# Two transformer layers on one core: second head's contexts of 19 steps turned by transfers, output products moved behind the next step's first projection

## The chip, the core and the metric

The kernel runs on one core of a Trainium2 chip. A core has five engines that run side by side, each taking its own instructions in order: TensorE (PE, matrix products and transposes; its weight loads are listed apart as PEld), VectorE (DVE), ScalarE (ACT), GpSimd (POOL) and SyncE (SP). SP does nothing here but start transfers; ACT and POOL can start transfers too. Transfers run on 16 DMA engines that all queues share. The metric is the device time of one execution in microseconds (us), lower is better. The kernel before takes 1981.68 us, the median of three runs (1981.44, 1981.68 and 1984.95).

## The reference, cut to what matters

Two layers, each `x = x + attention(layernorm(x)) + experts(layernorm(x))`, on 4 sequences of 512 tokens with 512 channels, all in float32. The change lies in the first layer, mostly in its attention:

```
q  = rope(rmsnorm(xn @ Wq))                  # 16 heads of 128
lk = rope(rmsnorm(xn @ Wlk)); lv = xn @ Wlv  # keys and values of the token's own window
ck, cv = compressed keys and values, one entry per 4 tokens
sc = q . ck                                  # only the 8 largest of each row are kept
ctx = (softmax(top8(sc)) @ cv + softmax(window(q . lk)) @ lv) / 2
out = concat_heads(ctx) @ Wo
...
ffn: each token goes to the 2 of 8 experts with the largest router logits
```

The output product `ctx @ Wo` sums over head and channel, so a context, which comes out with tokens on the partitions, has to be turned (channels on the partitions) before it can be the stationary operand of that product.

## The kernel before, in words

**Steps.** The first layer's attention runs in 32 steps `i`, one for each pair of heads `g` (8 of them) and sequence `b` (4). A step does the scores, the top 8, the contexts and the output products of its two heads, and beside them the projections of step `i + 1` (queries, keys and values, seven products in place of eight, after Strassen and Winograd). The main loop writes this by hand in program order:

- `scores(i, 0)`: compressed scores `sp` (L845), window scores `st` (L856), then exponentials (L860) on ACT, a mask (L864) on POOL and the top-8 chain (L848 to L880) on DVE. Then `turn_keys(1)` (L772).
- `first()` of the next step's projection: four products (L734, left operand from `wA`), their adds (L782, L788), then `finish(0)`: squares on ACT (L601), powers on POOL (L606), rotation on DVE (L613 to L616), scaling on ACT (L752).
- `scores(i, 1)`; `turn` of the first head's scores (L890, copies L891 and L892 on ACT); `second`; `context(i, 0)` (L906 to L924); `third`; `context(i, 1)`; `fourth` and `fifth`; the output products; and between them, at places `(i, h)`, jobs of other parts.

**Turning by PE or by transfer.** `turn_context` turns a context with four PE transposes (L931) into PSUM and copies it to `cT` on ACT (L932). From step 5 on the first head's context and half of the queries are turned by transfers instead: `split_halves` (L692, ACT, 1046 ns) parts each float32 into its high and low 16 bits, `store_halves` (L698) writes 256 KB to DRAM, and `load_halves` (L702) brings it back with a transposing transfer. The split tiles and the contexts share a tag `ctx` with two buffers.

**Output.** In steps 5 to 23 `output7` computes the output products of a step, again with seven products for eight (L970, 28 instructions), with four sums on DVE (L991 to L997) and seven adds into `acc` (L981). Its first part `before` is product x of the first head alone; `rest` starts with product y, which needs the second head. In the other steps `output` does it plainly (L939, L942). `load_out` (L108) loads `Wo` of a pair of heads into the only buffer, `combine_out` prepares the sums of `Wo` for `output7`.

**Other work in the steps.** Places in steps 2 to 4 hold the routing and, for every token tile `n` (16), `load_whole` (L1082), `part_halves` (L1087, ACT copy `xh<-xw`) and `store_parts` (L1090), which write the normalized rows to DRAM in halves. Places of steps 5 to 22 hold the experts, two blocks of 128 rows per step: `fetch_halves` (L524, POOL gathers the rows `xr`), `store_halves` of the experts (L529, `xrd`), `load_turned` (L534, transposing load `xT`), `fetch` (L489, POOL gathers the expert's weights `we`), `apply` (products L552, add L555, store `yd` L561). The last eight blocks hold two half blocks of 64 rows with an expert each and so fetch two sets of weights. In steps 29 to 31 the second layer's normalization of tiles 0 to 11 runs in the steps too (`next_layer`: L230 to L250, POOL add L1149, store of `acc` L1150).

**What sets the order.** The framework lays out each engine's instructions by a simulated timetable: it takes what it believes ready, the earlier in program order first. `tc.keep_in_program_order(x)` pins `x` behind the instruction written before it on the same engine; later instructions may still pass it. Transfers wait for their data at the head of the issuing queue, and everything behind them in that queue waits too. In these steps the projections and output products draw on three PSUM banks (`mm`), scores and contexts on three (`sc`).

Of the kernel before, what the change touches and what calls it, by code (L numbers as in the profile page):

```python
# [50 lines left out]
def two_layers(ctx: ExitStack, tc: tile.TileContext, a: dict, out: bass.AP, large: bass.AP):  # L51
# [54 lines left out]
    def load_out(g):  # L106
        wo = wpool.tile([P, HG, HID], F32, tag="Wo", name=f"Wo_{g}", bufs=1)
        nc.sync.dma_start(out=wo, in_=a["Wo"][ds(g * HG * D, HG * D), :].rearrange("(h p) c -> p h c", p=P))  # L108
        return wo
# [111 lines left out]
        tc.keep_in_program_order(V.memset(turned, 1.0))  # L221
        V.tensor_scalar(turned[R:P, :], wcol[R:P, 0:1], wcol[R:P, 1:2], D * math.sqrt(D), ALU.mult, ALU.mult)

    def layernorm(n, pool, bank, scaled=False, bufs=None):

# [13 lines left out]
        def rows():  # L241
            tag = "ctx" if n in (2, 3) else "xn"
            xn = made["xn"] = (wk0 if n in (2, 3) else pool).tile([P, HID], F32, tag=tag, name=f"xn_{n}", bufs=bufs)
            if scaled:
                pin(A.activation(xn, acc[:, n, :], AF.Identity, scale=mv[:, 1:2], bias=mv[:, 0:1]))
            else:
                made_ = V.tensor_scalar(xn, acc[:, n, :], mv[:, 0:1], mv[:, 1:2], ALU.subtract, ALU.mult)
                if n < TC or n + 1 == NT:
                    tc.keep_in_program_order(made_)
            (nc.scalar if TC <= n < 2 * TC else nc.sync).dma_start(out=xnd[ts(n, P), :], in_=xn)  # L250

        def turn():
            xn, tr = made["xn"], bank("tr", f"trx_{n}")
# [336 lines left out]
    for t_ in cv0s:  # L590
        G.memset(t_, 0.0)
        G.memset(t_[96:P, D : D + 1], 2.0)

    def squares(x, heads, pool, name, extra=1.0, use="k"):

# [436 lines left out]
    def first_logits(b):  # L1032
        def get(rows_):
            V.tensor_reduce(lg0[:, ts(b, TC), :], rows_[:, :, 1:, :], AX.X, ALU.add)
        row_w[b], turn = logits(b, wr, 1 + E, sp0, "r0", get, psum)
        return turn
# [41 lines left out]
    whole = {}  # L1078

    def load_whole(n):  # L1080
        x = whole[n] = rout["halves"].tile([P, HID], F32, tag="xw", name=f"xw_{n}", bufs=4)
        nc.sync.dma_start(out=x, in_=xnd[ts(n, P), :])  # L1082

    def part_halves(n):
        x = whole[n]
        xh = whole[n] = rout["halves"].tile([P, 2, HID], U16, tag="xh", name=f"xh_{n}", bufs=4)
        A.copy(xh, x.bitcast(U16).rearrange("p (d h) -> p h d", h=2))  # L1087

    def store_parts(n):
        tc.keep_in_program_order(nc.sync.dma_start(out=xhd[ts(n, P)], in_=whole.pop(n)))  # L1090
# [29 lines left out]
    for b, place in enumerate(((3, 4), (4, 0), (4, 1), (4, 2), (4, 3))):  # L1120
        if b:
            jobs0.append((place, lambda b=b: rout["r"].list(b - 1)))
        if b < B:
            jobs0.append((place, lambda b=b: rout["r"].mark(b)))
    there = [(2, 4)] + [(3, h) for h in (0, 1, 2, 3, 3.5, 4)] + [(4, h) for h in (0, 1, 2)]
    for n in range(NT):
        k = n // 2
        for d, f in enumerate((load_whole, part_halves, store_parts)):
            jobs0.append((there[k + d], lambda n=n, f=f: f(n)))
    jobs0.append(((4, 3), begin_experts))  # L1130
    jobs0.append(((4, 3.5), lambda: rout["ex"].store_halves(0)))
    jobs0.append(((4, 3.5), lambda: rout["ex"].fetch_halves(1)))
# [8 lines left out]
            jobs0.append((at[2 * i + 1], lambda i=i: rout["ex"].fetch(i + 1)))  # L1141
        jobs0.append((at[2 * i + 1], lambda i=i: rout["ex"].store_halves(i + 2)))
    def next_layer(n, pool, bank):
        make_rows, turn_ = layernorm(n, pool, bank, bufs=2 if bank is psum else TC)

        def rows():
            make_rows()

            G.tensor_tensor(acc[:, n, :], acc[:, n, :], rout["wo_b"], ALU.add)  # L1149
            nc.sync.dma_start(out=accd[ts(n, P), :], in_=acc[:, n, :])  # L1150
        return rows, turn_

    v = {}
# [129 lines left out]
    start[7][0]()  # L1283
    start[7][1]()
    first_logits(1)()
    for i, (g, b) in enumerate(steps):
        if b == 0:
            if g:
                out_w[g] = load_out(g)
            if g + 1 < NH // HG:  # L1290
                groups[g + 1] = load_later(g + 1)
        more = i + 1 < len(steps)
        turn_last = turn_keys
        now = qkT
        cT = qp.tile([P, HG, S], F32, tag="cT", name=f"cT_{g}_{b}", bufs=1)
        nc.sync.dma_start(out=cv0s[i % 2][96:P, 0:D], in_=cv[0:32, b, 0:D])
        em0, lT0 = scores(i, 0, now, (lambda: (turn_last(1), next(comp[0]))) if i == 0 else None)
        if i:
            turn_last(1)
        if more:  # L1300
            load_sums(i + 1)
            qkT, sums_x, first, second, third, fourth, fifth, turn_queries, turn_keys, _ = project(i + 1)
            first()
            sums_x()
            if b == 2 and g + 1 in groups:
                groups[g + 1][0][0] = load_block(g + 1, "wA")
        run0((i, 0))
        em1, lT1 = scores(i, 1, now)
        if i == 0:
            second(0)  # L1310
# [29 lines left out]
        if i >= 5:  # L1340
            load_halves(cT[:, 0:1, :].bitcast(U16), halves_c)
        ctx1 = context(i, 1, lT1, sT1, lv)
        if i < 5:
            turn_context(i, 0, ctx0, cT)
        if i == 5 or b == 0 and 5 < i < 24:
# [2 lines left out]
        if more:  # L1348
            fourth()


            if 5 <= i < 24:
                turn_queries(1)
                turn_keys(0)
                fifth()
            else:
                fifth()
        seven = 5 <= i < 24
        if seven:
            before, rest_ = output7(i, cT)  # L1360
            before()
        turn_context(i, 1, ctx1, cT)
        if more and not 5 <= i < 24:
            turn_queries(1)
            turn_keys(0)
        run0((i, 3.5))
        if seven:
            rest_()
        else:
            for t in range(TC):  # L1370
                output(i, t, cT)
        run0((i, 4))
# [1116 lines left out]
```

## Time and profile before

| what | value |
|---|---|
| median of 3 runs | 1981.68 us (1981.44 to 1984.95) |
| profiled execution | 1975.01 us, its span 1973.2 us |
| granted TensorE clock | 0.999 of full speed |
| PE busy | 1933.4 us, 98% of the span |
| DVE busy | 1481.5 us, 75% |
| ACT busy | 892.8 us, 45% |
| POOL busy | 756.1 us, 38% |
| context transposes L931 | 148 instructions, 23.7 us busy, 275 ns mean |
| `cT<-trc` copies L932 | 37, 576 ns mean |
| splits `halves_c<-ctx` L692 | 27, 1046 ns mean |
| transposing loads of `cT` L702 | 27, 3.2 us from issue to landing (median) |
| sum of PE's idle time, 300 to 1090 us (steps 5 to 23) | 7.35 of 790 us |

Steps 5 to 23 fill the time from about 280 to 1090 us, with a step every 43.1 us where nothing is disturbed. A busy time on PE is a latency from an instruction's start to its modelled end; instructions overlap, so how long PE is held by one is read from the start of the next. A bracket behind an instruction gives the time that its engine sat idle before it and what ended that. DMA rows give the time from issue to landing.

### The profile page before, as it was taken

The numbers are of one execution on the slowest core, as the hardware profiler recorded it, in microseconds if no ns is written. First come the engines' busy times: TensorE is split into PE (matmuls) and PEld (weight loads), VectorE is DVE, ScalarE is ACT, GpSimd is POOL, SyncE is SP. The second block draws the span as 40 slices with busy tenths as digits, with TensorE's granted clock in tenths as the row PEclk, the third lists the DMA queues.
The fourth block names the chain that finished last, engine by engine and source line by source line (L and its number), as shares of the span: only waits on it lengthen the run. The fifth ranks groups of instructions, "written<-read, shape, count | busy, mean of one in ns | idle before, by whom it ended". The sixth has DMA issues, their size and how long they took to land.

```text
span 1973.2 us, 28229 instructions
## 1 busy us (share of the span) xinstructions
PE 1933.4 (98%) x9010; PEld 1206.8 (61%) x9010; DVE 1481.5 (75%) x3662; ACT 892.8 (45%) x2650; POOL 756.1 (38%) x827
## 2 busy tenths in 40 slices
PE   7999999999999999999999999999999999999998
PEld 4676667776677677766667776666434445445443
DVE  7778878786776777776668888888796655666886
ACT  5556654444444444444445455455233433333332
POOL 5423244443433333344332454455114432333551
PEclk9999999999999999999999999999999999999999
DMA  9214366654666575567663433333317775775541
GB/s 293 104 61 142 130 176 180 198 155 144 186 191 167 172 204 152 147 184 223 221 223 98 121 109 109 95 113 105 122 53 257 256 256 191 277 251 175 158 154 67
DMA packets 224589, 326.51 MB, mean 165 GB/s; under 512 B 110384, under 2 KB 144304, under 8 KB 212656
## 3 DMA queue, kind: packets, MB, share of 16 engines
q1 hardware_dynamic: 196208, 173.60, 30.3%
q0 software_dynamic: 27072, 148.91, 22.4%
q10 hardware_dynamic: 1152, 2.10, 0.3%
q8 instruction: 74, 1.21, 0.3%
q14 instruction: 83, 0.68, 0.1%
HBM read 230.44 MB, written 70.25 MB: 152 GB/s over the span
## 4 chain that ended last, share of the span: by engine, by line
PE 79%; DVE 10%; DMA 4%; ACT 3%; issue 2%; POOL 1%; SPq 0%; DVEq 0%; ACTq 0%; POOLq 0%
PE p L734 23%; PE hp_r L552 12%; PE op L939 4%; PE st L856 4%; PE st L1522 3%; PE po L1660 3%; PE cx L1536 3%; PE qp L1498 3%; PE sp L845 2%; PE ox L970 2%; PE o L1605 2%; DMA halvesd_q<-halves_q 2%; PE oz L970 1%; PE ca L908 1%; PE trk L772 1%
## 5 line engine op out<-in xcount | busy, mean ns | idle before, releaser
L552 PE MATMUL hp_r<-we_r,xT_r 128*128 128x512 f32 (+1 forms) x592 | 226.4, 596 | 1.2 <-DMA we_r<-in_Wh,wrow_r 0.8
L606 POOL TENSOR_TENSOR ss_q<-ss_q,nhalf 128x4 f32<-128x4 f32 x64 | 70.9, 1108 | 375.0 <-ACT ss_q L603 375.0
L864 POOL TENSOR_TENSOR lT<-lT,lmask 128x512 f32<-128x512 f32 (+1 forms) x128 | 150.7, 1191 | 102.9 <-ACT lT L860 101.8
L734 PE MATMUL p<-wT,x 128*128 128x384 f32 x512 | 176.6, 488 | 2.6 <-DVE u L800 1.5
L734 PE MATMUL p<-wB,x 128*128 128x384 f32 x512 | 176.9, 490 | 1.3 <-DVE u L814 1.0
L734 PE MATMUL p<-wA,xnT 128*128 128x384 f32 x512 | 173.6, 490 | 1.0 <-DVE u L782 1.0
L860 ACT ACTIVATE lT<-st,ss_k 128x256 f32<-128x256 f32 (+1 forms) x256 | 98.8, 441 | 158.6 <-PE st L856 155.4
L1524 ACT ACTIVATE pT<-st 128x1024 f32<-128x1024 f32 x128 | 123.4, 1016 | 59.6 <-PE st L1522 51.1
L552 PEld LDWEIGHTS hp_r<-we_r,xT_r 128*128 128x128 f32 (+1 forms) x592 | 83.6, 170 | 98.2 <-issue 92.8
L734 PEld LDWEIGHTS p<-wB,x 128*128 128x128 f32 x512 | 94.0, 191 | 64.7 <-issue 8.8
L734 PEld LDWEIGHTS p<-wT,x 128*128 128x128 f32 x512 | 93.4, 190 | 64.9 <-DVE s L880 4.8
L734 PEld LDWEIGHTS p<-wA,xnT 128*128 128x128 f32 x512 | 95.1, 192 | 60.8 <-DVE u L782 2.8
L601 ACT ACTIVATE sq_q<-qb 128x128 f32<-128x128 f32 x256 | 79.2, 310 | 96.4 <-DVE qb L788 53.0
L856 PE MATMUL st<-qkT 128*128 128x256 f32 (+1 forms) x512 | 114.6, 353 | 0.0
L569 POOL DMA_INDIRECT row_r<-yd,slot_r x64 | 72.5, 1133 | 74.5 <-DMA yd<-yr_r 21.8
L856 PEld LDWEIGHTS st<-qkT 128*128 128x128 f32 x512 | 92.2, 190 | 11.5 <-issue 1.8
L939 PE MATMUL op<-Wo,cT 128*128 128x512 f32 x208 | 92.8, 593 | 0.0
L752 ACT ACTIVATE qb<-qb,ss_q 128x128 f32<-128x128 f32 x256 | 81.8, 392 | 21.3 <-POOL ss_k L605 16.0
L606 POOL TENSOR_TENSOR ss_k<-ss_k,nhalf 128x2 f32<-128x2 f32 (+1 forms) x96 | 86.7, 903 | 8.0
L734 PE MATMUL p<-wT,xnT 128*128 128x384 f32 x256 | 88.2, 487 | 0.3 <-DVE wT L121 0.3
L489 POOL DMA_INDIRECT xr_r<-xnd,rows_r x36 | 40.5, 1125 | 120.6 <-PE trm_r L540 88.4
L922 ACT ACTIVATE ctx<-cb,sums 128x128 f32<-128x128 f32 x128 | 39.7, 360 | 101.0 <-DVE sums L918 93.6
(390 smaller groups left out, 4558.5 us busy)
## 6 DMA issues: line engine op xcount, KB each, us to landing
x<-xsd SPq DMA_DIRECT2D x112, 256.0 KB, 5.1
yd<-yr_r SPq DMA_DIRECT2D x72, 256.0 KB, 5.4
xrd_r<-xr_r SPq DMA_DIRECT2D x36, 256.0 KB, 2.3
halvesd_c<-halves_c SPq DMA_DIRECT2D x27, 256.0 KB, 3.5
halvesd_q<-halves_q SPq DMA_DIRECT2D x26, 256.0 KB, 2.9
wA<-in_wA SPq DMA_DIRECT2D x16, 384.0 KB, 3.8
wB<-in_wB SPq DMA_DIRECT2D x16, 384.0 KB, 6.8
xnd<-xn SPq DMA_DIRECT2D x24, 256.0 KB, 2.0
```

Source lines behind the costliest of these rows:

```text
L552: PE.matmul(hp[ts(h, m), :], lhsT=xT[:, k, ts(h, m)], rhs=w[:, ts(k, HID)], start=(k == 0), stop=(k == KC - 1))
L569: G.indirect_dma_start(out=x, out_offset=None, in_=self.yd, in_offset=at_rows(self.r.slot[:, k, n : n + 1]))
L601: pin(A.activation(sq, x[:, h, :], AF.Square, accum_out=ss[:, j : j + 1]))
L606: pin(G.tensor_tensor(ss, ss, nhalf[:, 0:n], ALU.pow))
L734: fixed(PE.matmul(p, lhsT=x[:, k, ts(c, P)], rhs=w[:, k, :], start=(k == 0), stop=(k == 1)))
L752: A.activation(x[:, j, :], x[:, j, :], AF.Copy, scale=scale[:, n : n + 1])
L856: PE.matmul(st[:, ds((t % 2) * 256, n)], lhsT=qkT[:, HG + h, ts(t, P)], rhs=qkT[:, h, ds(t * P, n)], start=True, stop=True)
L860: A.activation(lT[:, ds(half * 512 + c * 256, n)], st[:, ds(c * 256, n)], AF.Exp, scale=norm_k[(i, h)][2 * half + c])
L864: G.tensor_tensor(dst, dst, lmask.rearrange("p a w j -> p (a w j)")[:, 0:n], ALU.mult)
L939: PE.matmul(op, lhsT=cT[:, h, ts(t, P)], rhs=wo[:, h, :], start=(h == 0), stop=(h == HG - 1))
L970: PE.matmul(p[:, ts(c, 256)], lhsT=left[:, ts(c, P)], rhs=right, start=new and c == 0, stop=True, skip_group_check=True)
L1524: A.activation(pt[:, ts(pair, 2), :], st, AF.Exp, scale=SCALE1)
```

## The change

From step 5 to 23 the second head's context is split on ACT (`c1`), stored and loaded back turned into `cT[:, 1]`, as the first head's already was. The products of `output7` and the load that they need are kept in a list `before_this` and put behind the next step's `first()`. `load_out` goes behind them. The 16 KB copy of the first compressed entries is written behind `first()` for the next step (from step 4 on), just ahead of the transposing load. `xw` and `xh` of tiles 0 to 5 are worked in steps 1 and 2 in an earlier pool, the others in steps 2 to 4, and the ACT copies are pinned. In steps 29 to 31 the two stores of `next_layer` are issued by ACT.

```
-    def layernorm(n, pool, bank, scaled=False, bufs=None):
+    def layernorm(n, pool, bank, scaled=False, bufs=None, on_scalar=False):
...
-            (nc.scalar if TC <= n < 2 * TC else nc.sync).dma_start(out=xnd[ts(n, P), :], in_=xn)
+            (nc.scalar if TC <= n < 2 * TC or on_scalar else nc.sync).dma_start(out=xnd[ts(n, P), :], in_=xn)
...
+    def load_first_entries(i):
+        nc.sync.dma_start(out=cv0s[i % 2][96:P, 0:D], in_=cv[0:32, steps[i][1], 0:D])
...
     def load_whole(n):
-        x = whole[n] = rout["halves"].tile([P, HID], F32, tag="xw", name=f"xw_{n}", bufs=4)
+        x = whole[n] = (rout["halves"] if n >= 6 else sp0).tile([P, HID], F32, tag="xw", name=f"xw_{n}", bufs=4 if n >= 6 else 2)
...
-        A.copy(xh, x.bitcast(U16).rearrange("p (d h) -> p h d", h=2))
+        tc.keep_in_program_order(A.copy(xh, x.bitcast(U16).rearrange("p (d h) -> p h d", h=2)))
...
-    there = [(2, 4)] + [(3, h) for h in (0, 1, 2, 3, 3.5, 4)] + [(4, h) for h in (0, 1, 2)]
+    there = [((1, 4), (2, 0), (2, 1)), ((2, 0), (2, 1), (2, 2)), ((2, 1), (2, 2), (2, 3)), ((2, 4), (3, 0), (3, 1)),
+             ((3, 0), (3, 1), (3, 2)), ((3, 1), (3, 2), (3, 3)), ((3, 4), (4, 0), (4, 1)), ((4, 0), (4, 1), (4, 2))]
     for n in range(NT):
-        k = n // 2
-        for d, f in enumerate((load_whole, part_halves, store_parts)):
-            jobs0.append((there[k + d], lambda n=n, f=f: f(n)))
+        for place, f in zip(there[n // 2], (load_whole, part_halves, store_parts)):
+            jobs0.append((place, lambda n=n, f=f: f(n)))
...
-        make_rows, turn_ = layernorm(n, pool, bank, bufs=2 if bank is psum else TC)
+        make_rows, turn_ = layernorm(n, pool, bank, bufs=2 if bank is psum else TC, on_scalar=bank is psum)
...
-            nc.sync.dma_start(out=accd[ts(n, P), :], in_=acc[:, n, :])
+            (nc.scalar if bank is psum else nc.sync).dma_start(out=accd[ts(n, P), :], in_=acc[:, n, :])
...
+    before_this = []
     for i, (g, b) in enumerate(steps):
         if b == 0:
-            if g:
-                out_w[g] = load_out(g)
...
-        cT = qp.tile([P, HG, S], F32, tag="cT", name=f"cT_{g}_{b}", bufs=1)
-        nc.sync.dma_start(out=cv0s[i % 2][96:P, 0:D], in_=cv[0:32, b, 0:D])
+        if i < 5:
+            load_first_entries(i)
...
+            if i >= 4:
+                load_first_entries(i + 1)
+        if before_this:
+            load_halves(cT[:, 1:2, :].bitcast(U16), before_this[0])
+        for f in before_this[1:]:
+            f()
+        before_this = []
+        cT = qp.tile([P, HG, S], F32, tag="cT", name=f"cT_{g}_{b}", bufs=1)
         run0((i, 0))
+        if g and b == 0:
+            out_w[g] = load_out(g)
...
         ctx1 = context(i, 1, lT1, sT1, lv)
+        seven = 5 <= i < 24
+        if seven:
+            halves_c = split_halves(f"c1_{i}", ctx1.bitcast(U16).rearrange("p n (f x) -> p n x f", x=2))
...
         if seven:
-            before, rest_ = output7(i, cT)
-            before()
-        turn_context(i, 1, ctx1, cT)
-        if more and not 5 <= i < 24:
-            turn_queries(1)
-            turn_keys(0)
+            before_this = [store_halves(f"c1_{i}", halves_c), *output7(i, cT)]
+        else:
+            turn_context(i, 1, ctx1, cT)
+            if more:
+                turn_queries(1)
+                turn_keys(0)
         run0((i, 3.5))
-        if seven:
-            rest_()
-        else:
+        if not seven:
             for t in range(TC):
                 output(i, t, cT)
```

## The prediction

> **What bounds the kernel now.** I read the page first, then the stretch of steps 5 to 23 by windows, the PE's timeline over one turn from step to step, and last the PE's own waits.
>
> The page's busy list and chain, and the window of steps 5 to 23 (columns: stretch, length, then PE, PEld, DVE, ACT, POOL busy with counts, clock, DMA share, GB/s):
>
> ```profile
> PE 1933.4 (98%) x9010; PEld 1206.8 (61%) x9010; DVE 1481.5 (75%) x3662; ACT 892.8 (45%) x2650; POOL 756.1 (38%) x827
> ...
> PE 79%; DVE 10%; DMA 4%; ACT 3%; issue 2%; POOL 1%; SPq 0%; DVEq 0%; ACTq 0%; POOLq 0%
> ...
> 300.00:1090.00 790.00, 782.65 (x3653) 551.96 (x3652) 595.31 (x1616) 362.75 (x1269) 296.20 (x315) 1.00 0.60 177
> ```
>
> PE idles 7.35 of 790 us at full clock: every instruction taken from PE there shortens the kernel, every new PE wait lengthens it. The turn from step 12 to 13 (start, length, instruction):
>
> ```profile
> 602.57 2.75 PE L734 MATMUL p<-wB,x 128*128 128x384 f32 x8
> 605.15 1.03 PE L970 MATMUL ox<-Wo,cT 128*128 128x256 f32 x4
> 606.01 0.60 PE L931 MATMUL trc<-ident,ctx 128*128 128x128 f32 x4
> 606.45 1.06 PE L845 MATMUL sp<-ckT,qkT 128*128 128x32 f32 x8
> ...
> 614.48 5.33 PE L734 MATMUL p<-wA,xnT 128*128 128x384 f32 x16
> ```
>
> The second head's four transposes hold PE from 606.01 to 606.45, and PE goes on without a gap. The PE waits that matter (in brackets):
>
> ```profile
> 211.95 0.33 PE L931 MATMUL trc<-ident,ctx 128*128 128x128 f32 x1 [2.38 <-DVE ctx L924]
> ...
> 465.33 0.71 PE L911 MATMUL cb<-cv,sT 96*128 96x129 f32 x4 [1.27 <-ACT sT L891]
> ...
> 990.79 0.71 PE L911 MATMUL cb<-cv,sT 96*128 96x129 f32 x4 [2.17 <-ACT sT L891]
> ...
> 1305.27 0.63 PE L255 MATMUL trx<-ident,xn 128*128 128x128 f32 x4 [3.55 <-DVE xn L247]
> ```
>
> **Transposes removed.** 19 x 4. The L931 row says 275 ns each, and the Trainium skill ("TensorE: Matmul & The Clock Gate", Part 4: PE-mode transpose) also gives about 275 ns in a kernel; that would be 76 x 0.275 = 20.9 us. But this is a latency: start to start, four take 0.44 us. So 19 x 0.435 = **-8.3 us**, and the timeline decides, since PE is full. The copy out of PSUM (0.57 us, ACT) goes; a split into halves (1.05 us, the L692 row) comes. It starts when ctx1 is done at 599.5, in an ACT gap of 3.47 us before 602.33: nothing.
>
> **The transfers.** Frame: that same turn. SP's queue:
>
> ```profile
> 600.13 0.34 SPq L561 DMA_DIRECT2D yd<-yr_r  x1
> 601.10 0.34 SPq L529 DMA_DIRECT2D xrd_r<-xr_r  x1
> 601.89 3.77 SPq L685 DMA_DIRECT2D x<-xsd  x2
> 607.70 1.27 SPq L534 DMA_TRANSPOSE xT_r<-xrd_r  x1
> ```
>
> The new store is pinned behind xrd: issue about 601.5, some 1.2 us after POOL's weight gather began at 600.37. Stores whose issue ends up to 0.94 us after a gather's start land in 2 to 4 us; those ending 0.97 to 1.6 after it land with the gather, in 6.2, 6.7 and 7.4 us (xrd at 385.2, 298.7, 730.4). The Trainium skill ("DMA: Bandwidth & Descriptors", Queues, rings and completion order) says that a DMA engine round-robins between rings by packet, which would let a small store through in about 3 us; its remark that a completion waits for that engine's earlier writes in all queues fits the slow rows better. I take the rows: landed near 608.2, then the transposing load at the cT row's median 3.2 us: **611.4**. SP sits at its wait meanwhile; behind it are the x loads (next read over 20 us later) and xT_r (landing about 614, read at 621.6).
>
> Who needs it: product y. After fifth's end at 605.15 come sp 0.89, st 1.52, keys 0.44, first 5.16 and product x 0.86: **614.0**. Slack 2.6 us, no wait in steps with one weight gather per expert. In steps 18 to 21 a second gather (half experts) delays stores to 8.9 and 10.1 us (xrd at 952.8 and 999.1); there the data come up to 2 us late: +2.5 us in all (ends 0 and +6). By the packet rule it would be 0, and the sum 2.5 lower.
>
> **The products moved.** Same 28 instructions, 6.0 us, now behind first. Their DVE work (seven adds, four sums, 6.3 us) moves from 606-614 to 613-622. DVE must then do some 13.0 us in the 15.2 us up to 628.4 (products 6.3, rotation 1.5, second head's top-8 chain 3.1, the rest 2.1), while the first head's chain runs earlier, uncovered. Full, not over: +1 us in all (ends 0 and +10). Wo's load, now behind the products, waits at SP until about 619 instead of 613; nothing follows it before 626.7, its reader combine_out is later still. The first-entry copies (16 KB, 2.2 us) sit ahead of the transposing load and are ready early: nothing.
>
> **What moves with it on POOL.** The row gather (L524) is pinned behind the pow of first's finish, which comes 6.5 us earlier, so the gather goes from 624.4 to about 617.8 and xrd no longer waits for it:
>
> ```profile
> SPq L529 <- DMA xr_r<-xhd,rows_r: 35.5, 30, 2.6
> ...
> ACT halves_c L692 <- DMA halvesd_q<-halves_q: 22.1, 4, 6.2
> ```
>
> The second row is the cause of the four PE waits at L911 (6.0 us): the query store landed with the weight gather, ACT held the split and sT behind it. From the four, PE waits once that store lands more than about 14.7 us after the first head's score transposes (463.9 - 448.05 = 15.8 gave 1.27). After the change it issues 1.4 us earlier, but so does the gather, and the store ends about 1.0 us after the gather's start, on the border. If slow, it lands 7.1 to 9.3 us after 626.4, by 635.7; the limit is 621.6 + 14.7 = 636.3. So no new wait, and most old ones go: **-5.0 us** (ends 0 and -6.0).
>
> **Step 3.** Twelve xh copies (1.05 us) lie on ACT there; squares wait, then L616, then ctx. PE loses 2.38 + 0.19 + 0.58, and the granted clock falls to 0.60 and 0.55 in 214 to 218, another 1.7: 4.9 us. The change leaves six in step 3, pinned behind the squares, and puts six in step 2, where ACT is busy 23.4 of 42.0 us. I take **-4.0** (0 to -4.9).
>
> **Steps 29 to 31.** At 1294.6 SP waits 2 us for POOL's add before the accd store, the query store behind it lands at about 1300.4, ACT's split waits, and PE loses 3.55. On ACT's queue that store (0.33 us each, 24 issues, 8 us of an ACT that is half idle) no longer delays SP. The squares still need their own time: **-2.0** (ends -3.6 and +3, if ACT stands at POOL's add).
>
> **Sum**: -8.3 - 4.0 - 2.0 - 5.0 + 2.5 + 1.0 = -15.8 us. The profiled execution has span 1973.2 and 1.8 around it, 1975.0; it would be 1959.2. The median of the runs is 6.7 higher, 1981.68, and I move it by the same: **1965.9 us**.
>
> **Rivals.**
> - *The second head's data come late in every step* (slower). Against: 2.6 us of slack by medians. For: a store has taken 9.3 us beside one gather (454.5) and a transposing load 4.9; 601.5 + 9.3 + 4.9 = 615.7, 1.7 us late. PE waits in order: 19 x 1.7 = 32 us, sum +16: **1998**. It decides from 15.8 / 19 = 0.83 us per step, and a wait of over 2 us may also lower the clock as in step 3.
> - *Only the transposes go.* The order is laid out anew, the waits of steps 3 and 29 and at L911 reappear elsewhere: -8.3 + 3.5 = -4.8: **1977**. For: these waits are accidents of order.
> - *DVE bounds the moved stretch.* For: 609 to 615 already shows DVE busy 6.00 of 6. Against: POOL and PE leave room until 628. 0.4 us per step is +7.6: **1973.5**.
>
> **How the numbers follow.** Mine 0.50 (own range 1960 to 1973), nothing lost in the half-expert steps 0.05 (1960), DVE 0.12, transposes only 0.15, late data 0.18 (1985 to 2000 mostly). 0.2% of 1981.7, 4 us, is about what a measurement can tell from no change. Faster: 0.55 + 0.10 + 0.08 = 0.73; same 0.09; slower 0.18. The range 1957 to 1988 leaves out some 0.13 above and 0.05 below.
>
> **What would show it.** No L931 in steps 5 to 23, L931's count down by 76; first score transposes about 42.7 us apart instead of 43.1; no PE wait at L970's oy above 0.3 us in full-expert steps; transposing loads of cT at 46, landing about 3.2 us after issue; L911's waits under 1.5 us in total; no low clock near 215. Waits of PE at L970 on a DMA, or at L734 on DVE, in most steps would make me wrong.

## The result, and the profile after

The changed kernel takes 2074.45 us (median of four runs, 2072.66 to 2078.05) where the kernel before, on the same chip, takes 1981.56 (1979.04 to 1984.95): a ratio of 1.0468, 95% interval 1.0447 to 1.0489. It is 93 us slower; the forecast was 16 us faster. Its profiled execution has a span of 2072.0 us.

The page's busy list, and the windows of the stretch that the changed kernel has between step 5 and step 23 (columns as in the prediction):

```profile
PE 1964.5 (95%) x8934; PEld 1214.8 (59%) x8934; DVE 1492.7 (72%) x3662; ACT 909.6 (44%) x2650; POOL 748.7 (36%) x827
...
297.00:1186.00 889.00, 811.84 (x3576) 557.82 (x3576) 603.90 (x1623) 379.59 (x1273) 291.44 (x317) 0.96 0.58 168
```

PE has 76 instructions fewer, as the change says, and is busy 31 us longer. In the stretch it idles 77 us, where it idled 7, and its clock is 0.96, where it was 1.00. Lines after L593 have moved down by 3 to 10: the projections' product is L737 (was L734), first's adds L785 and L791, the contexts' products L914 (was L911), the output products L973 (was L970), the four sums of `output7` L994 to L1000.

What PE and DVE wait for (us in total, times, longest):

```profile
PE p L737 <- DVE u L785: 65.8, 20, 6.4
PE cb L914 <- ACT sT L894: 8.5, 6, 2.1
...
DVE cS L994 <- DMA cT<-halvesd_c: 84.7, 18, 7.9
```

So DVE waits for the second head's turned context, and PE waits for DVE. Now the turn that the prediction followed; `fifth` ends at 639.22 in this kernel, 34.1 us later than the 605.15 of the prediction's frame. SP's queue:

```profile
636.36 0.34 SPq L529 DMA_DIRECT2D xrd_r<-xr_r  x1
637.15 0.38 SPq L701 DMA_DIRECT2D halvesd_c<-halves_c  x1
...
644.20 1.20 SPq L705 DMA_TRANSPOSE cT<-halvesd_c  x1
```

SP stands at the turning load until the store has landed, 7.05 us after its issue. DVE in the same turn:

```profile
643.01 0.28 DVE L880 MATCH_REPLACE8 rep<-top,s 128x128 f32<-128x128 f32 x1
647.72 0.43 DVE L994 TENSOR_TENSOR cS<-cT 128x256 f32<-128x256 f32 x1 [4.43 <-DMA cT<-halvesd_c]
648.06 0.48 DVE L882 TENSOR_TENSOR rep<-s,rep 128x320 f32<-128x320 f32 x1
648.46 0.55 DVE L785 TENSOR_TENSOR u<-p,b 128x384 f32<-128x384 f32 x1
```

And PE:

```profile
642.71 3.39 PE L737 MATMUL p<-wA,xnT 128*128 128x384 f32 x10
649.07 2.93 PE L737 MATMUL p<-wA,xnT 128*128 128x384 f32 x4 [2.97 <-DVE u L785]
651.79 1.91 PE L973 MATMUL ox<-Wo,cT 128*128 128x256 f32 x4
653.50 1.81 PE L973 MATMUL oy<-Wo,cT 128*128 128x256 f32 x4
655.14 1.03 PE L973 MATMUL ow<-WoT,cT 128*128 128x256 f32 x4
```

This is the whole mechanism. The context lands at 647.7, which is 613.6 in the frame of the prediction: 2.2 us later than forecast and 0.4 us ahead of product y as forecast (614.0). But DVE wants it first: the sum `s1 = a21 + a22` (L994) needs no product, so the laid-out order has it ahead of the end of the first head's top-8 chain and ahead of first's bias adds. DVE stands at it for 4.43 us. First's fourth product then finds its three `mm` banks full, PE stands 2.97 us, and after that the clock is low. The windows before, in and after the dip:

```profile
640.00:649.00 9.00, 6.10 (x27) 3.89 (x25) 4.26 (x21) 3.25 (x11) 3.67 (x4) 0.96 0.79 216
649.00:653.00 4.00, 3.93 (x7) 2.52 (x8) 3.28 (x9) 1.59 (x7) 0.00 (x0) 0.50 0.08 29
```

The three groups from 649.07 to 655.14 hold PE for 6.07 us; with the sum pinned (below), at full clock, the same three take 3.13 (612.44 to 615.57). A wait of 2.97 us costs nearly as much again. Over the execution: 65.8 us waited at L737, and clock 0.981 of 2072.0 against 0.999 of 1973.2 is another 37 us; with the transposes' 8.3 off, that is 95 of the 98.8 us by which the two spans differ.

**Where it sits.** The table gives, for the profiled execution of each kernel told of below, the length of some stretches between the first score transposes of one step and those of another (L893, was L890; step k is the stretch that ends at step k's), and the median of the steps 6 to 19. Each row is a single execution. That of the kernel before was a quick one (1975.0 us, clock 0.999; its 70 runs beside the experiments took 1972.8 to 1988.1 us, clock 0.998 to 0.992), so a difference of some us between two rows can be the clock of one execution.

| kernel | steps 3-5 | 6-19 | median step | 20-23 (half experts) | step 30 |
|---|---|---|---|---|---|
| before | 126.8 | 605.7 | 43.12 | 183.4 | 42.8 |
| changed | 121.5 | 676.2 | 48.25 | 212.0 | 44.1 |
| side parts alone | 121.4 | 603.6 | 43.12 | 184.7 | 45.7 |
| products moved, turned on PE | 121.4 | 618.7 | 43.67 | 192.2 | 44.1 |
| weight gather later | 121.3 | 634.7 | 45.06 | 188.9 | 45.4 |
| sum pinned | 121.3 | 613.4 | 43.17 | 185.0 | 45.8 |
| sum pinned, store on ACT | 121.7 | 614.2 | 43.17 | 195.1 | 44.3 |
| sum pinned, adds first | 121.3 | 614.0 | 42.91 | 196.6 | 45.5 |
| both of these | 121.6 | 606.3 | 42.68 | 195.3 | 44.4 |
| and all half stores on ACT | 121.5 | 597.7 | 42.68 | 185.5 | 43.5 |
| and three steps on PE | 122.1 | 598.0 | 42.68 | 174.8 | 43.5 |
| and row stores on SP | 122.0 | 598.4 | 42.68 | 176.1 | 40.8 |
| the last without the pin | 121.5 | 692.2 | 49.56 | 177.9 | 40.7 |
| before, some half stores on ACT | 124.6 | 604.7 | 43.12 | 196.9 | 40.2 |

### The profile page after: what moved, and what is told of

It reads as the page before. It is cut to its first block, busy times and chain, and to the rows that moved or that the text cites. A ratio compares the mean times of both kernels' runs of the same rounds, so it can differ in the third digit from the quotient of the medians.

```text
span 2072.0 us, 28192 instructions
## 1 busy us (share of the span) xinstructions
PE 1964.5 (95%) x8934; PEld 1214.8 (59%) x8934; DVE 1492.7 (72%) x3662; ACT 909.6 (44%) x2650; POOL 748.7 (36%) x827
## 5 line engine op out<-in xcount | busy, mean ns | idle before, releaser
L737 PE MATMUL p<-wA,xnT 128*128 128x384 f32 x512 | 196.0, 525 | 65.8 <-DVE u L785 65.8
L737 PE MATMUL p<-wT,x 128*128 128x384 f32 x512 | 176.8, 488 | 1.7 <-DVE wT L121 1.1
L737 PE MATMUL p<-wB,x 128*128 128x384 f32 x512 | 176.0, 488 | 0.9 <-DVE yr_r L555 0.9
L737 PEld LDWEIGHTS p<-wA,xnT 128*128 128x128 f32 x512 | 97.1, 202 | 130.1 <-DVE u L785 78.5
L737 PEld LDWEIGHTS p<-wB,x 128*128 128x128 f32 x512 | 93.7, 190 | 64.8 <-issue 8.4
L737 PEld LDWEIGHTS p<-wT,x 128*128 128x128 f32 x512 | 93.3, 190 | 63.7 <-DVE s L883 4.8
L884 ACT ACTIVATE s<-s 128x320 f32<-128x320 f32 x64 | 30.1, 471 | 205.5 <-DVE s L883 205.5
L859 PE MATMUL st<-qkT 128*128 128x256 f32 (+1 forms) x512 | 108.7, 354 | 1.0 <-DVE s L851 0.7
L737 PE MATMUL p<-wT,xnT 128*128 128x384 f32 x256 | 88.1, 487 | 0.3 <-DVE wT L121 0.3
```

Of the source, the lines that this page charges most:

```text
L737: fixed(PE.matmul(p, lhsT=x[:, k, ts(c, P)], rhs=w[:, k, :], start=(k == 0), stop=(k == 1)))
L859: PE.matmul(st[:, ds((t % 2) * 256, n)], lhsT=qkT[:, HG + h, ts(t, P)], rhs=qkT[:, h, ds(t * P, n)], start=True, stop=True)
```

## The experiments

None of these kernels leaves out work. The kernel before was run beside each group; its medians there were 1979.3 to 1980.7.

**The sum pinned.** My theory on seeing the trace: the transfer is late for one DVE instruction only, and that one stands in the wrong place.

```
-            V.tensor_tensor(s1, a21, a22, ALU.add)
+            tc.keep_in_program_order(V.tensor_tensor(s1, a21, a22, ALU.add))
```

> The changed kernel with one addition: the first of output7's four sums (cS = cT of head pair, the only DVE instruction before product y that reads the second head's turned context) is pinned on DVE behind the add of product x. No wait, transfer or amount of work is removed. Theory A (order on DVE): the transfer is late only for that sum, which stands ahead of first's bias adds; PE waits through them. Then the 17 waits of PE at L737 for DVE's add (65.8 us) vanish with the low clock that follows them, PE's busy time falls by about 39 us, and the time is the one that I forecast by the sum, 1958 to 1972 us; product y on PE waits under 0.5 us per step. Theory B (the turned context is late for PE as well): the waits move to product y at L973, 1 to 4 us in each step, and the time stays between 1998 and 2060. Theory C (DVE has too much to do in the stretch): PE still waits for DVE at L737 or at L973, time 2000 to 2070.

Measured: 1985.71 us (ratio to before 1.0033, interval 1.0018 to 1.0048). One pin takes 88.7 of the 92.9 us away (by the medians); no transfer has become faster by it: in step 13 the turning load is issued 6.95 us after the store, before 7.05. The sum now waits for the context once, 0.3 us, where DVE waited 84.7 us. That is theory A, and B and C fall as causes of the loss. But the time isn't the one that the sum gave: 20 us are still missing. PE's waits:

```profile
PE cb L914 <- ACT sT L894: 7.1, 5, 2.3
PE p L737 <- DVE u L785: 6.1, 19, 1.7
PE oy L973 <- DMA cT<-halvesd_c: 3.5, 3, 1.8
```

The second row is a wait of 0.21 to 0.50 us in 17 steps, besides one of 1.7 in step 30. Step 13 on DVE, and on PE:

```profile
609.45 1.27 DVE L882 TENSOR_TENSOR rep<-s,rep 128x320 f32<-128x320 f32 x1
610.75 1.17 DVE L883 SCALAR_TENSOR_TENSOR s<-rep,s 128x320 f32<-128x320 f32 x1
611.84 0.55 DVE L785 TENSOR_TENSOR u<-p,b 128x384 f32<-128x384 f32 x1
...
616.24 0.42 DVE L994 TENSOR_TENSOR cS<-cT 128x256 f32<-128x256 f32 x1
```

```profile
608.84 3.39 PE L737 MATMUL p<-wA,xnT 128*128 128x384 f32 x10
612.44 1.56 PE L737 MATMUL p<-wA,xnT 128*128 128x384 f32 x4 [0.21 <-DVE u L785]
```

First's first add comes behind the end of the top-8 chain, and 0.21 us too late for the fourth product. It costs more than the wait itself: from 608.84 to the start of product x at 613.84 first's last fourteen matmuls hold PE 5.00 us, and in one piece 4.51 (adds first, below). These 0.5 us in a step are all that the transposes gave: the steps are 43.17 us long, before 43.12.

**The side parts alone.** The transposes, the products and `Wo`'s load are as before; the edits of `xw` and `xh`, the row stores on ACT and the early copies of first entries stay.

```
-            before_this = [store_halves(f"c1_{i}", halves_c), *output7(i, cT)]
+            before, rest_ = output7(i, cT)
+            before()
...
+        turn_context(i, 1, ctx1, cT)
...
+        if seven:
+            rest_()
```

> The side parts alone: the xw and xh tiles of the first six blocks in their own buffers and places, the stores of the row passes on ACT's queue, the copies of the first entries ahead. Transposes, products and Wo's load are where the kernel before has them. My sum gives -4.0 (step 3) and -2.0 (steps 29 to 31): 1975.6 us. If these waits are accidents that reappear elsewhere (the rival that only the transposes go): 1979 to 1983. If a part of the loss sits here (theory D: the queue of ACT carries the stores badly): over 1985, with PE waits at L254 to L264 or in the last steps.

Measured: 1976.49 us (ratio 0.9985, interval 0.9971 to 0.9999). By the table steps 3 to 5 gain 5.4 us, a little more than forecast, and step 30 loses 2.9: PE's lines of it, where the kernel before has one wait of 3.55 us:

```profile
1300.39 1.09 PE L255 MATMUL trx<-ident,xn 128*128 128x128 f32 x4 [2.23 <-DVE xn L247]
...
1324.87 1.56 PE L737 MATMUL p<-wA,xnT 128*128 128x384 f32 x4 [1.70 <-DVE u L785]
```

The wait that I took for removed has become two. And the clock falls behind the first of them, to 0.50 from 1300.4 to 1303.8, which it did not behind the longer wait of the kernel before (1.00 from 1305 to 1309).

**The products moved, turned on PE.** The changed kernel without the store and load of the second head.

```
+        turn_context(i, 1, ctx1, cT)
         if seven:
-            before_this = [store_halves(f"c1_{i}", halves_c), *output7(i, cT)]
+            before_this = [*output7(i, cT)]
```

> The changed kernel with the second head's contexts turned on PE at their old place instead of by transfers; the products stay moved behind the next step's first projection. Theory A: no datum comes late, so no PE wait for DVE at L737 over 0.5 us, and the time is that of the side parts alone within 4 us, with the gain at L914's waits still in it: about 1970 to 1978. Theory C (the moved products overload DVE's stretch): most of the loss stays, 2010 to 2070. The move alone costing a little (0.4 us per step, my DVE rival): about 1978 to 1983.

Measured: 1991.66 us (ratio 1.0051, interval 1.0033 to 1.0070). With no transfer there is no long wait, so the move as such isn't the 93 us. But it costs more than I had allowed, 15.2 us over the side parts alone (1976.49). Full-expert steps take 43.67 us in place of 43.12, in gaps too small for the list of waits. In step 13, 0.33 of it is at first's last fourteen matmuls (4.84 us in place of 4.51), the rest at the output products, where DVE is late with giving banks back:

```profile
618.80 1.03 PE L973 MATMUL ow<-WoT,cT 128*128 128x256 f32 x4
619.73 1.13 PE L973 MATMUL ox<-WoT,cS 128*128 128x256 f32 x4
620.70 0.55 PE L848 MATMUL sp<-ckT,qkT 128*128 128x32 f32 x4
```

`ow` holds PE for 0.93 us in place of 0.86, `ox` for 0.97. Steps 20 to 23 take 192.2 us, before 183.4, though no second context is transferred: PE waits 6.7 us for `sT` there (3.10, 1.71 and 1.91), and the clock falls behind each. The pinned kernel's 43.17 is 0.5 us less than 43.67, about what the transposes held PE; the two kernels differ in DVE's order too, so this is no clean measure of them.

**The weight gather later.** The changed kernel, unpinned, with the weight gather of each step's second slot issued behind the store of the second head's context:

```
-            jobs0.append((at[2 * i + 1], lambda i=i: rout["ex"].fetch(i + 1)))
+            second_ = at[2 * i + 1][1] == 3
+            jobs0.append(((at[2 * i + 1][0], 3.5) if second_ else at[2 * i + 1], lambda i=i, p=second_: rout["ex"].fetch(i + 1, p)))
```

(`fetch(..., p)` pins the gather on POOL.)

> The changed kernel, with POOL's weight gather of each step's second slot issued after the second head's context is stored instead of 2 us before it; DVE's order is as the planner then lays it out. It tests what makes the transfer late. If the store lands late because it shares the engines with the gather: the store of the second head's context lands 2 to 4 us after issue instead of 7, the turned context is there some 3 to 4 us earlier (about 644 where it was 647.7), DVE's first sum waits 0 to 3 us, PE's waits at L737 shrink to under 20 us in all, time 1965 to 2000. If the store is slow by itself (its descriptors, the write's receipt): it still lands 6 to 7 us after issue, and the time stays above 2050. The weights then land some 4 us later; they are read over 10 us after that, so nothing is expected from them (a PE wait at their reader would be a cost of this experiment alone).

Measured: 2016.77 us (ratio 1.0186, interval 1.0167 to 1.0205). In step 13 the turning load is issued 2.57 us after the store, not 7.05, and in all nineteen steps after 2.3 to 4.0 us, so the store was slow by its company. DVE's first sum waits 8.2 us for `cT` in all, where it waited 84.7. PE's waits for first's add (L787 in this kernel) fall to 15.7 us. I had forecast 1965 to 2000, and the time misses that, for a reason of this kernel alone (DVE, then POOL):

```profile
621.90 0.43 DVE L996 TENSOR_TENSOR cS<-cT 128x256 f32<-128x256 f32 x1
622.26 3.28 DVE L884 TENSOR_TENSOR rep<-s,rep 128x320 f32<-128x320 f32 x1
625.46 0.54 DVE L787 TENSOR_TENSOR u<-p,b 128x384 f32<-128x384 f32 x1
```

```profile
621.88 1.05 POOL L489 DMA_INDIRECT we_r<-in_Wex,wrow_r  x1 [0.20 <-DVE rep L882]
622.96 2.22 POOL L869 TENSOR_TENSOR lT<-lT,lmask 128x512 f32<-128x512 f32 x2
```

The moved gather pushes POOL's masks (L869) on top of the end of the chain and the sums. Here the comparison takes 3.28 us; the shortest of its kind takes 0.48. In each of the steps 6 to 22 at least one DVE instruction with two operands in SBUF takes 1.9 to 4.3 us over both masks. PE waits 1.26 us behind the comparison in step 13.

**Two separate repairs of what was left.** To the pinned kernel, first, the second head's store on ACT's queue behind its split:

```
             halves_c = split_halves(f"c1_{i}", ...)
+            halves_c = store_halves(f"c1_{i}", halves_c, nc.scalar)
```

> The kernel with the pinned sum, with the second head's store on ACT's queue right behind its split, not on SP's behind the routed rows' store: it is issued some 1.5 us earlier, when the weight gather has just begun. The pinned-sum kernel left 6 us of loss against the kernel before. If late data make it (theory L): its three PE waits for cT at L973 (0.53, 1.15, 1.84 us) go, and the steps that they lengthened with them, 4 to 7 us: 1978 to 1982. If the place of first's adds behind the first head's top-8 chain makes it (theory O, 0.21 us of wait and as much of drain in each of 19 steps), full-expert steps stay at 43.16 us each and the time falls by 0 to 4: 1982 to 1986.

Measured: 1991.67 us (ratio 1.0054, interval 1.0039 to 1.0070), worse than both forecasts. In full-expert steps the turning load now starts 3 to 5 us after the store in place of 4 to 9, yet they stay at 43.17: late data don't set them, the order does. In half-expert steps the load can start only 11 to 12 us after the store, PE's waits for `cT` grow to 7.9 us and those at L914 to 10.5 (why the latter grow, no run tells).

Second, to the pinned kernel, first's adds ahead of the end of the chain: `scores` gives back its last two masking instructions as a function, and `first` calls it after its third add.

```
                 fixed(V.tensor_tensor(u2[:, c, :], made.pop(0), b2[:, 0, :], ALU.add))
+                if picked and c == 1:
+                    picked()
```

> The kernel with the pinned sum, with first's adds laid ahead of the end of the first head's top-8 chain on DVE: the two masking instructions (L882, L883 of the changed kernel, which took 1.27 + 1.17 us beside POOL's mask of lT) are pinned behind the third of first's four adds. The store is where the changed kernel has it. Theory O: the 0.21 us waits of PE at L737 and the drain behind them go, full-expert steps fall from 43.16 to about 42.7 us, 19 x 0.45 = 8.5 us in all: 1975 to 1979. Theory D (DVE has too much in this stretch, whatever the order): the wait moves to a product at L973 or to the score transposes at L893, and the time stays at 1983 to 1990.

Measured: 1990.82 us (ratio 1.0048, interval 1.0032 to 1.0065). The time missed its forecast and the mechanism met it. DVE and PE in step 13 (L785 and L793 are first's adds, L886 is the comparison):

```profile
617.39 0.56 DVE L785 TENSOR_TENSOR u<-p,b 128x384 f32<-128x384 f32 x1 [0.73 <-PE p L737]
617.87 0.48 DVE L886 TENSOR_TENSOR rep<-s,rep 128x320 f32<-128x320 f32 x1
```

```profile
613.97 4.68 PE L737 MATMUL p<-wA,xnT 128*128 128x384 f32 x14
```

DVE now waits for PE, fourteen products run in one piece, and an undisturbed step (6 of the 14) takes 42.68 us, which is 0.43 less than before: the 0.435 of the sum. The gain is lost again at product y (L980 here), seven waits for `cT`, 14.0 us, four of them in full-expert steps. Product y comes sooner, the store is where it was, and what had hidden its lateness is gone.

Both together:

> Both of the above together. If they are independent, the sum of the two gains over the pinned-sum kernel's 1985.7: 1969 to 1976, which is about what I had predicted for the change. If only the order counts: 1976 to 1980.

Measured: 1986.61 us (ratio 1.0031, interval 1.0016 to 1.0046). Full-expert steps have 42.68 us where nothing waits, but steps 20 to 23 take 195.3 us where the kernel before needs 183.4. The adds gain in the full-expert steps; the loss left is in these four: waits for `sT` (1.15, 1.72 and 2.46 us) and for `cT` at product y (3.08 and 4.44), with 13.7 us at half clock behind them.

**All half stores on ACT's queue.** In addition the queries' and the first head's stores are issued by ACT, each right behind its split.

```
-                halves_q = split_q()
+                halves_q = store_halves(f"q_{i}", split_q(), nc.scalar)
...
             halves_c = split_halves(f"c_{i}", ...)
+            halves_c = store_halves(f"c_{i}", halves_c, nc.scalar)
```

> As the kernel with the store and the adds moved, and the stores of the queries' and of the first head's contexts' halves on ACT's queue as well, each right behind its split (SP had them behind the next context, the routed rows and the x loads). It tests what makes PE wait at L914 for sT (7.1 us in 5 waits with the pinned sum, 6.0 in 4 before): the query store lands late, ACT's split of the first head's contexts waits for its buffer, and sT stands behind it on ACT. If so, earlier query stores take these waits to under 2 us and the clock dips behind them: 6 to 10 us less than the kernel without, 1962 to 1970. If the issues on ACT (three of 0.35 us per step) hold up ACT's chain, PE waits for ACT at L893, L911 or L914 grow and the time is over 1980.

Measured: 1969.97 us (ratio 0.9951, interval 0.9925 to 0.9978; ten runs, 1961.04 to 1987.95): the first with the second head's transfers that beats the kernel before. The list has no wait at the contexts' products for `sT` any more, and full-expert steps are 42.68 us long almost without exception. ACT's wait for the query store ahead of its next split, 65.3 us in the kernel without (17 times), is gone as well. So those waits came from late half stores, as the prediction says; the queries' and the first head's moved together, so this run doesn't part the two. What is left is in half-expert steps (list of waits; the three are in steps 20 to 22):

```profile
PE oy L980 <- DMA cT<-halvesd_c: 7.7, 3, 3.1
```

**Three steps on PE again, and the row stores on SP.** The contexts of steps 19 to 21 are turned by PE; then also the row passes' stores go back to SP's queue.

```
+        by_pe = 19 <= i < 22
-        if seven:
+        if seven and not by_pe:
             halves_c = split_halves(f"c1_{i}", ...)
...
+            if by_pe:
+                turn_context(i, 1, ctx1, cT)
```

> The best kernel so far (sum pinned, adds first, all half stores on ACT's queue), with the second head's contexts of steps 19, 20 and 21 turned on PE again, where two weight gathers per slot kept its store for 12.5 to 13.3 us and PE waited for cT at L980 (2.49, 3.10, 2.12 us). If these waits and the clock dips behind them are what the half-expert steps lose, the three steps fall from 46.1, 49.7 and 46.1 us to 44 to 45 each: 7 to 10 us less than without, 1960 to 1964. If something else holds these steps (the gathers themselves, the half blocks' arithmetic), they stay and the time stays near 1970.

```
-            (nc.scalar if TC <= n < 2 * TC or on_scalar else nc.sync).dma_start(out=xnd[ts(n, P), :], in_=xn)
+            (nc.scalar if TC <= n < 2 * TC else nc.sync).dma_start(out=xnd[ts(n, P), :], in_=xn)
...
-            (nc.scalar if bank is psum else nc.sync).dma_start(out=accd[ts(n, P), :], in_=acc[:, n, :])
+            nc.sync.dma_start(out=accd[ts(n, P), :], in_=acc[:, n, :])
```

> The same, with the row passes' stores (normalized rows and sums of the last group) on SP's queue again as in the kernel before. My prediction gave their place on ACT's queue a gain of 2.0 us in steps 29 to 31; the step tables so far show the opposite, 43.5 to 45.8 us for the step from 29 to 30 where the kernel before has 42.8. If that is the stores' doing, the time falls by 1 to 3 us against the kernel with them on ACT; if my sum was right, it rises by 2.

Measured: 1956.04 us (ratio 0.9875, interval 0.9849 to 0.9901), and with the row stores on SP 1953.53 (ratio 0.9867, interval 0.9844 to 0.9891). The three steps fall to 43.8 us each, so the late context was most of what they had lost, and more than I expected comes back. With the row stores back on SP's queue the time is 2.5 us lower by the medians (the ranges of the four runs of each overlap by 0.5) and step 30 takes 40.8 us in place of 43.5. The fastest kernel's steps 6 to 23, by its window:

```profile
270.00:1040.00 770.00, 769.47 (x3549) 537.20 (x3548) 572.04 (x1589) 377.43 (x1262) 294.11 (x322) 1.00 0.69 195
```

PE idles 0.5 of 770 us.

**The kernel before with these stores alone.** Nothing of the change, only the queries' and the first head's half stores on ACT's queue, by the same lines as above.

> The kernel before, with only the queries' and the first head's contexts' half stores on ACT's queue, each right behind its split; nothing of the change. It tells how much of the best kernel's gain is this alone. The four waits at L911 (6.0 us) and what the clock loses behind them should go, the steps from 5 to 23 stay at 43.11: 6 to 8 us less than before, 1973 to 1976. If the store place also serves the routed blocks in the other steps, lower. If the three issues cost ACT's chain something, no change: 1980.

Measured: 1986.50 us (ratio 1.0047, interval 1.0023 to 1.0072). The full-expert steps keep their 43.12 us and the waits at L911 shrink to 1.6 us, but in steps 20 and 21 the first head's context is late (list of waits):

```profile
PE ox L970 <- DMA cT<-halvesd_c: 12.0, 2, 7.0
```

These two steps take 52.4 and 53.9 us. So the stores on ACT alone aren't what made the fastest kernel, and they are a risk by themselves wherever two weight gathers run.

**The fastest kernel without the pin.** Does a store that starts early make the pin needless?

```
-            tc.keep_in_program_order(V.tensor_tensor(s1, a21, a22, ALU.add))
+            V.tensor_tensor(s1, a21, a22, ALU.add)
```

> The best kernel (1953.5 us) with the pin of the first sum taken away again, nothing else. It asks whether a store that starts early makes the pin needless. In the laid-out order the unpinned sum (L1001 here) then stands on DVE even ahead of the first head's top-8 chain. If the order decides, DVE stands at that sum until the turned context lands, some 10 us after the store's issue, with the chain and first's adds behind it: PE waits at L737 for L785 by 3 to 5 us in each step with a transfer (16 of them), the clock falls behind each wait, and the time is 2020 to 2090. If early data is enough, the sum waits under 1 us and the time stays at 1953 to 1965.

Measured: 2047.45 us (ratio 1.0344, interval 1.0315 to 1.0374). It doesn't. DVE's and PE's first rows, and step 13 on each:

```profile
PE trk L775 <- DVE top L881: 52.1, 10, 7.4
PE p L737 <- DVE u L785: 11.5, 5, 3.9
...
DVE cS L1001 <- DMA cT<-halvesd_c: 72.2, 15, 7.9
```

```profile
648.87 0.96 DVE L1001 TENSOR_TENSOR cS<-cT 128x256 f32<-128x256 f32 x1 [4.29 <-DMA cT<-halvesd_c]
```

```profile
651.44 1.09 PE L775 MATMUL trk<-ident,lv 128*128 128x128 f32 x4 [4.40 <-DVE top L881]
```

The layout moved the sum even further forward, ahead of the chain, so the wait is as long as in the changed kernel. The place where PE meets it is another, the turned keys (L775, not L737 as I had written), whose rotation also stands behind the sum; the size is the forecast one.

## Why the prediction was wrong

**The step that failed** is "Who needs it: product y ... 614.0. Slack 2.6 us, no wait". I looked for the first reader of the turned context among PE's instructions. Its first reader is the sum on DVE, which depends on no product, and the layout had put it 4 us ahead of the data: DVE stood at it for 84.7 us in 18 waits, and PE behind DVE for 65.8. The pin of that one instruction took back 88.7 of 92.9 us, and taking the pin away from another kernel brought 94 us back. The trace before had shown the sum ahead of product y already (DVE, then PE):

```profile
607.35 0.43 DVE L991 TENSOR_TENSOR cS<-cT 128x256 f32<-128x256 f32 x1
...
607.78 1.03 PE L970 MATMUL oy<-Wo,cT 128*128 128x256 f32 x4
```

**The landing time** was out by 2.2 us: 611.4 forecast, 613.6 measured, most of it because the store was issued at 603.1 and not at 601.5. The store took 7.05 us, as the rows of stores behind a gather said and not as the packet rule would have it. For the loss this didn't matter. But the slack of 2.6 us was 0.4 in this turn, and "no wait in steps with one weight gather" didn't hold either: with the sum pinned and the adds first PE reached product y when forecast (8.88 us after `fifth`'s end, 8.87 forecast) and waited for it in four full-expert steps, 0.54 to 2.98 us.

**The slower rival** had the right sign and subject and the wrong place and price. I let PE wait for product y, 1.7 us in each step, 32 us in all. The wait was on DVE, with first's adds behind it, up to 6.4 us, and I gave the clock half a sentence: it cost about 37 us beside 65.8 waited. The text's last part does name "L734 on DVE, in most steps" as what would make it wrong; its price was nowhere in the sum.

**Transposes, -8.3:** right. An undisturbed step is 0.43 us shorter, 0.435 forecast, once nothing stands in the way.

**DVE, +1.0 with ends 0 and +10:** under-sized. Moving the products put the top-8 chain and the sums ahead of first's adds; that costs about 0.5 us per step (43.67 against 43.12 without transfers, 43.17 against 42.68 with them), some 9 us. The move alone lost 15.2 us by the medians, with the half-expert steps. I had written that the chain "runs earlier, uncovered" and charged nothing for it. What bounds isn't how busy DVE is, as the rival had it: with the same instructions in another order the loss was gone.

**Half-expert steps, +2.5:** under-sized. With everything else repaired, three waits of 2.12 to 3.10 us for the late context, and 6.8 us at half clock behind one of them, cost steps 20 to 23 10.7 us (185.5 against 174.8 with these contexts turned on PE).

**L911, -5.0:** wrong. The waits stayed (8.5 us in the changed kernel, 7.1 with the pin). I had put the query store "on the border" of being late and taken the good side. Their cause was named rightly, and it grew: the row that the prediction shows with 22.1 us, 4 times, is after the change:

```profile
ACT halves_c L695 <- DMA halvesd_q<-halves_q: 50.3, 14, 6.1
```

**Step 3, -4.0:** right (5.3 in steps 3 to 5). **Steps 29 to 31, -2.0:** wrong sign: step 30 is 2.9 us longer with the side parts alone, as one wait of 3.55 us became one of 2.23 and one of 1.70, with 3.4 us at half clock. What does shorten the old wait, to 1.0 us, is that the queries' and the first head's stores leave SP's queue: with that alone step 30 takes 40.2 us, where before it took 42.8.

Repaired, the change ends below what its sum had promised, 1953.53 us against 1965.9. That doesn't confirm the sum: the repairs (the pin, the adds first, all half stores on ACT, three steps on PE, the row stores on SP) also took away waits of the kernel before that the sum had left in, and the clock's falls with them, so that four runs lie within 1.7 us.

## What to carry to other kernels

When a transfer takes an operand's place, list every reader of it on every engine and find where each stands in that engine's queue; an in-order engine waits at the first of them, with all that is behind it. Where a tool lays out the order by what it believes of a transfer, pin the first reader behind the last thing that mustn't wait for it. And price a PE wait of 2.5 us and more with the low clock that will mostly follow it, 1.7 to 3.4 us more (counts below).

## What the hardware showed that I hadn't expected

**A PE wait brings the clock down by chance, and more surely the longer it is.** In all fourteen traces the granted clock is either 1.00 or 0.50. I counted the PE waits of 1 us and more between 70 and 1950 us, and those with a stretch at 0.50 that begins during the wait or within 3.5 us of its end: none of 23 waits under 1.5 us, 17 of 69 from 1.5 to 2.5, 12 of 13 from 2.5 to 3.5, 23 of 24 above. Such a stretch lasts 3.41, 6.83 or 10.24 us (half of it is lost), and in each trace the starts are whole multiples of 3.41 us apart, whatever the waits. So where a wait falls on this raster decides too: the 3.55 us of the kernel before went free, 2.23 us in the side parts' kernel did not. The changed kernel has twelve stretches, 68 us together.

**A comparison on DVE stretches beside POOL.** `rep<-s,rep` (128x320, two operands in SBUF) takes 0.48 us at least and up to 3.28. In the pinned kernel 38 of the 64 overlap one of POOL's masks of `lT`: their median is 1268 ns, that of the other 26 is 492. With the adds first, where it runs some 4 us later, 19 overlap one, the median over 64 is 491 ns, and DVE's busy time falls from 1496.3 to 1469.0 us. The Trainium skill ("SBUF — State Buffer", Who interferes with whom) says that a DVE instruction with two SBUF inputs contends with a GpSimd instruction that reads SBUF, and that the order of issue decides which of them blocks; the 3.28 us that end 0.36 us behind a mask pair of 2.22 fit. The order was changed in these runs, not the mask alone, so the port as the cause is argued, not shown.

**Beside two gathers the queue of a store matters less than its place.** In the half-expert steps the turning load starts 11 to 13 us after a store on ACT's queue and 9 to 12 after one on SP's, but the store on ACT is issued 1 to 2 us sooner. Counted from the issue of the second weight gather the load starts after 11.3 to 12.6 us with the store on SP (three kernels) and 11.8 to 13.6 on ACT (three kernels), so it comes when the gathers are through, on either queue; in the kernel with all half stores on ACT the second gather lands 1.5 or 1.6 us before the store. One store on ACT slipped ahead of both gathers, in the kernel with the store and the adds moved. Its load starts 3.67 us later and PE doesn't wait, where a step earlier the load starts 13.13 us after the store:

```profile
951.64 0.94 POOL L489 DMA_INDIRECT we_r<-in_Wh,wrow_r  x1 [0.30 <-issue]
952.15 0.38 ACTq L701 DMA_DIRECT2D halvesd_c<-halves_c  x1
965.28 1.20 SPq L705 DMA_TRANSPOSE cT<-halvesd_c  x1
...
1004.60 0.38 ACTq L701 DMA_DIRECT2D halvesd_c<-halves_c  x1
1005.30 0.94 POOL L489 DMA_INDIRECT we_r<-in_Wex,wrow_r  x1 [2.77 <-PE hp_r L552]
1006.55 0.94 POOL L489 DMA_INDIRECT we_r<-in_Wh,wrow_r  x1 [0.30 <-PE p L737]
1008.27 6.11 SPq L705 DMA_TRANSPOSE cT<-halvesd_c  x1
```

In full-expert steps the store on ACT comes both sooner (0.2 us after the gather's issue in most) and on another queue, and its load starts after about 3 us; which of the two does it, these runs don't part.
